# Random-feature attention and a mixture of experts on one core: phases of the feature map computed in bfloat16 parts, with all range reduction on TensorE

## The chip, the cores and the metric

One core of a Trainium2 chip runs the whole program; seven other cores idle. The metric is the device time of one execution in microseconds (us); the lower the better. Before the change the median of six runs is 532.13 us (530.05 to 541.41). A matmul on TensorE (PE) reads its stationary operand by a weight load (PEld) and streams the other; results go to PSUM, which VectorE (DVE) and ScalarE (ACT) empty. GpSimd (POOL) does small work and issues the indirect transfers; SyncE (SP) issues most other transfers.

## The reference

Eight sequences of 512 rows and 128 columns pass attention with 16 heads of 8, a layer norm, a mixture of 8 experts of which each row uses 2, and a second layer norm. All is float32.

```python
def _fourier_kernel(x, proj_mat):
    p = jnp.einsum('blhd,dm->blhm', x, proj_mat) / math.sqrt(D_HEAD)
    return jnp.concatenate([jnp.cos(p), jnp.sin(p)], axis=-1) / math.sqrt(D_KMAP)
q = (x @ Wq.T + bq).reshape(Bv, Lv, N_HEAD, D_HEAD)      # D_HEAD = 8
...
q_prime = _fourier_kernel(q, proj_mat)                    # 128 + 128 features a head
k_prime = _fourier_kernel(k, proj_mat)
kv = jnp.einsum('blhm,blhd->bhmd', k_prime, v)
out = jnp.einsum('blhm,bhmd->blhd', q_prime, kv)
...
x = _layernorm(x + attention(x)); x = _layernorm(x + experts(x))
```

The experts: `relu(x @ W1[e] + b1[e]) @ W2[e] + b2[e]`, weighted by a softmax over the two best of the router's logits.

## The kernel before

**Steps.** The attention of a sequence is cut into 8 steps, 64 in all. Steps 0 to 3 are key steps: each takes 128 rows, and computes the phases p of all 16 heads (128 x 2048 values, in turns: the scale holds a factor 1/(2 pi)), their sines and cosines into a tile `f`, and from them the products with the values (`bank<-f,vm`). After the fourth the sums are transposed into `kv`. Steps 4 to 7 are query steps: each takes 4 heads and all 512 rows, phases again, then `bank<-f,kv`.

**Phases** (`p_phase`, line 546). Keys and queries stand as `kT`, `qT` with (head, dimension) on 128 partitions, in float32. `pbd` holds the projection as a block matrix over 4 heads (32 rows). Four float32 matmuls in four row groups of 32 write four PSUM banks, tiles `p` (two tiles of two banks, line 171). There is one such set: the next step's phases wait until this set is read.

**Range reduction.** A sine needs its argument within half a turn. The constant `TURNED` (line 1476) lists the steps, 0 to 23, in which TensorE does it: after the phases it adds and subtracts a large constant by eight bfloat16 matmuls (`p<-up,once`, `p<-down,once`), so that the bank holds the rounded phase, and subtracts the phases by a second set of float32 matmuls with `npbd`, the negated table. What remains in `p` is minus the fraction. DVE then takes absolute values (`v_abs`, `f<-p` on DVE, two halves) and ACT sines (`v_sin`, `f<-p` on ACT, two halves), and the bank is free. In the other 40 steps ACT rounds (`v_round`, `r<-p,magic`, two halves), DVE subtracts (`v_turn`, `r<-r,p`, two halves), which frees the bank, and from `r` DVE takes absolute values (`f<-r`) and ACT sines (`f<-r`). In both kinds ACT makes the cosines from the absolute values (`f<-f,halfpi`). Two `f` and two `r` tiles exist.

**Experts.** After a sequence's attention its rows are normalized, routed, and scattered by POOL to pages of 128 rows by expert in DRAM (`ys<-y,slot_i`). Pages must first be cleared: SP writes `zero` to them (`ys<-zero`, 19 MB, in the steps 1 to 16). Sequences 0 to 5 form a first group of 55 tiles, 6 and 7 a second of 23. Each tile: SP loads the page (`yg`, 64.5 KB) and the expert's weights (`wst<-wcat`, 322 KB, 6 buffers); TensorE transposes four pages at once (`ident,yg`), does `p_hidden` (`yTg,wst`, four float32 matmuls that the profile counts as eight) and `p_answers` (`w,hT`, likewise); DVE does `hT` and `og` between and after; POOL scatters the answers (`res<-og,yg`). When a group's answers are all there, they are fetched, weighted, normalized and stored.

**The order of the work.** Class `Plan` (line 1342) lays out every task in program order at build time by a list schedule: a task has an engine, an estimated time, predecessors, buffers, and a due time, shifted by kind (`SHIFT`, line 1478). The hardware then runs each engine's instructions strictly in that order (`InOrder`, line 70). All instructions are issued in one helper, so that the profile gives line 78 for nearly all; groups are told apart by the tiles they name. Each class of work uses four PSUM banks (`bank`); after the last step the four phase banks serve too.

Of the kernel before, what the change touches and what calls it, by code (L numbers as in the profile page):

```python
# [18 lines left out]
ROUND = 12582912.0  # L19
# [6 lines left out]
def kernel(  # L26
# [65 lines left out]
    wpool = ctx.enter_context(tc.tile_pool(name="wpool", bufs=6))  # L92
# [24 lines left out]
    first = feat.tile([P, NG * 512], F32, tag="r", name="first")  # L117
    wnat = first[:, 0 : 4 * D].rearrange("p (i d) -> p i d", d=D)
    for i, w in ((1, Wk), (0, Wq), (2, Wv), (3, Wo)):
        nc.scalar.dma_start(out=wnat[:, i, :], in_=w)  # L120
    proj_s = first[0:DH, 4 * D : 4 * D + M]
    sp.dma_start(out=proj_s, in_=proj)
    NB = E * NF
    brow = first[0 : NB + 3, 4 * D + M : 4 * D + M + P]
# [35 lines left out]
    pbd = const.tile([P, NJ * M], F32, name="pbd")  # L160


    npbd = const.tile([P, NJ * M], F32, name="npbd")
# [15 lines left out]
    )  # L179
    mm(P4[3][:, 0:M], heads, proj_s, start=True, stop=True)  # L180
# [11 lines left out]
    bqk = const.tile([P, 2], F32, name="bqk")  # L192


    def p_bcol(bank):
        tr(bank[:, 0 : NB + 3], brow, ident[: NB + 3, : NB + 3])

    def v_bcol(bank):
        dve.tensor_copy(bcol, bank[:, 0 : NB + 3])
        dve.tensor_scalar(bqk, bcol[:, NB : NB + 2], scale, None, ALU.mult)  # L200
# [19 lines left out]

    XW = D + DH
    vm = const.tile([P, NC, NJ * XW], F32, name="vm")
    pool.memset(vm, 0.0)
    kv = const.tile([P, 2, NJ * XW], F32, name="kv")
    pool.memset(kv, 0.0)
# [30 lines left out]
    DY = D + 1  # L258
    zero = const.tile([P, 8, DY], F32, name="zero")
    pool.memset(zero, 0.0)  # L260
    pool.memset(zero[:, :, D:DY].bitcast(I32), 1 << 30)
# [17 lines left out]
    def clear(i, e):  # L279
        n = full[i] if e + 1 < E else NT[i]  # L280
        for t0 in range(0, n, 8):
            k = min(8, n - t0)
            r0 = P * (full[i] * e + t0)
            sp.dma_start(
                out=ys_d[i][r0 : r0 + k * P, :].rearrange("(p k) d -> p k d", k=k),
                in_=zero[:, 0:k, :],
            )
# [56 lines left out]
    class Inverse:  # L344
# [5 lines left out]
        def tile(self, tag):  # L350
            return small.tile([P, NC], F32, tag=tag, name=f"{tag}_{self.name}")
# [8 lines left out]
        def newton(self, eng):  # L360

            rs, ve = self.rs, self.ve
            nw = self.tile("nw")
            eng.tensor_tensor(nw, rs, rs, ALU.mult)
# [61 lines left out]
    def v_rows(bank, r):  # L426
        if r == 0:
            rows8.append(feat.tile([P, NG * 512], F32, tag="r", name="rows8"))
        dve.tensor_copy(rows8[0][:, NG * r * D : NG * (r + 1) * D], bank)
# [7 lines left out]
    def prepare_shift():  # L437
# [10 lines left out]
        for r in range(E // NG):  # L448
# [3 lines left out]
                bank=("rows", r), free=("rows", r), ring=("r", "rows", 2),  # L452
# [3 lines left out]
        plan.give("r", "rows", [t], lag=5)  # L456
        return t

    wr_done, bcol_done = [], []

    def prepare_logits():
        t = plan.add("PE", 0.2, p_bcol, kind="p_bcol", due=-3.5, bank="bcol")
        b = plan.add("DVE", 0.45, v_bcol, kind="v_bcol", due=-3.4, after=[t], bank="bcol", free="bcol")
        bcol_done.append(b)
        t = plan.add("PE", 0.2, p_wo, kind="p_wo", due=-0.5, bank="wo")
# [5 lines left out]
    class Sequence:  # L471
        def __init__(self, b):
# [5 lines left out]
            self.xb = self.z = None  # L478

# [20 lines left out]
        def p_qk(self, i, bank):  # L500
            mm(bank, wT[:, i, 0:D], self.xT, start=True, stop=True)

        def v_qk(self, i, bank, eng):
            t = seq.tile(
                [P, L], F32, tag="qk"[i] + "T", name=f"{'qk'[i]}T_{self.b}", bufs=2 - i
            )
            if eng is dve:
                dve.tensor_scalar(
                    t, bank, bcol[:, NB + i : NB + i + 1], scale, ALU.add, ALU.mult
                )  # L510
            else:
                act.activation(t, bank, AF.Identity, bias=bqk[:, i : i + 1], scale=scale)
            if i:
                self.kT = t
            else:
                self.qT = t
# [29 lines left out]
        def p_phase(self, i, turned):  # L546
            for g in range(NG):
                r0 = 32 * g
                if i < NC:
                    lhs, rhs = self.kT[r0 : r0 + 32, ts(i)], pbd[r0 : r0 + 32, :]  # L550
                else:
                    lhs, rhs = pbd[r0 : r0 + 32, ts(i - NC)], self.qT[r0 : r0 + 32, :]
                mm(P4[g], lhs, rhs, start=True, stop=not turned)
# [13 lines left out]
            for g in range(NG):  # L567
                r0 = 32 * g
                if i < NC:
                    lhs, rhs = self.kT[r0 : r0 + 32, ts(i)], npbd[r0 : r0 + 32, :]  # L570
                else:
                    lhs, rhs = npbd[r0 : r0 + 32, ts(i - NC)], self.qT[r0 : r0 + 32, :]
                mm(P4[g], lhs, rhs, start=False, stop=True)
# [54 lines left out]
        def v_z(self, n, bank):  # L628
            if n == 0:
                self.z = seq.tile([P, NC, D + E], F32, tag="z", name=f"z_{self.b}")  # L630
                self.mv = small.tile([P, NC, 2], F32, tag="mv", name=f"mv_{self.b}")
# [181 lines left out]
        def start_out(self):  # L813
            self.mvo = small.tile([P, NC, 2], F32, tag="mvo", name=f"mvo_{self.b}")
# [5 lines left out]
        def prepare(self):  # L820
# [6 lines left out]
            else:  # L827
# [12 lines left out]
            self.t_k = add("PE", 1.0, lambda bank: self.p_qk(1, bank), kind="p_qk1", due=due + 1, after=[e] + ([before.t_p[NC - 1]] if b else []), bank=("k", b))  # L840
            self.k_done = add(
                "DVE", 0.75, lambda bank: self.v_qk(1, bank, dve), kind="v_qk1", other=("ACT", 0.7, lambda bank: self.v_qk(1, bank, act)), due=due + 1.3,
                after=[self.t_k] + bcol_done, bank=("k", b), free=("k", b),
            )
            self.t_v, self.v_done = [], []
            for n in range(2):
# [9 lines left out]
            self.t_q = add("PE", 1.0, lambda bank: self.p_qk(0, bank), kind="p_qk0", due=due + 4, after=[e] + ([seqs[b - 2].t_p[NS - 1]] if b > 1 else []), bank=("q", b))  # L856
            self.q_done = add(
                "ACT", 0.7, lambda bank: self.v_qk(0, bank, act), kind="v_qk0", other=("DVE", 0.75, lambda bank: self.v_qk(0, bank, dve)), due=due + 4.3,
                after=[self.t_q] + bcol_done,
                bank=("q", b), free=("q", b),  # L860
            )

        def steps(self):
            add = plan.add
            self.t_p, self.t_products = [], []
            for i in range(NS):
                k = NS * self.b + i
                turned = k in TURNED
                s = Step(self, i, turned)
                p = add(  # L870
                    "PE", 2.5 if turned else 1.1, s.p_phase, kind="p_phase", due=k,
                    after=[self.k_done if i < NC else self.q_done], take="p", step=k,
                )
                self.t_p.append(p)
                if turned:
                    a0 = add("DVE", 1.2, lambda s=s: s.v_abs(0), kind="v_abs", due=k + 0.1, after=[p], ring=("f", k, 2))
                    s0 = add("ACT", 1.05, lambda s=s: s.v_sin(1), kind="v_sin", due=k + 0.1, after=[p], ring=("f", k, 2))
                    a1 = add("DVE", 1.2, lambda s=s: s.v_abs(1), kind="v_abs", due=k + 0.1, after=[a0, s0])
                    s1 = add("ACT", 1.05, lambda s=s: s.v_sin(0), kind="v_sin", due=k + 0.1, after=[a0, s0])
# [4 lines left out]
                else:  # L884
                    r0 = add("ACT", 1.1, lambda s=s: s.v_round(0), kind="v_round", due=k + 0.05, after=[p], ring=("r", k, 2))
# [4 lines left out]
                    a = add("DVE", 1.25, lambda s=s: s.v_absolute(), kind="v_absolute", due=k + 1.0, after=[d1], ring=("f", k, 2))  # L890
                    sin = add("ACT", 1.92, lambda s=s: s.v_sine(), kind="v_sine", due=k + 1.2, after=[d1], ring=("f", k, 2))
                    plan.give("r", k, [a, sin])
# [5 lines left out]
                c0 = add("PE", 1.05, lambda bank, s=s: s.p_products(0, bank), kind="p_products", due=k + 2.3, after=sins + need, bank=key)  # L898
                c1 = add("PE", 1.05, lambda bank, s=s: s.p_products(1, bank), kind="p_products", due=k + 2.4, after=[cos, c0], bank=key)
# [5 lines left out]
        def plan_kv(self):  # L905
# [5 lines left out]
                "DVE", 0.6, self.v_kv, kind="v_kv", due=k + 0.5,  # L911
# [618 lines left out]
```

## Time and profile before

| what | us |
|---|---|
| median of six runs | 532.13 |
| the profiled execution | 527.6 |
| its span, first to last instruction | 525.6 |
| first phase matmul | 11.2 |
| steps 0 to 23 (first phase of step 24) | to 146.7 |
| last product of the attention | 397.3 |
| last matmul | 502.8 |
| PE busy | 464.4 |
| DVE busy | 397.2 |
| ACT busy | 358.6 |
| POOL busy | 279.0 |

Busy times are sums over the span; engines work side by side. A row of the profile gives line, engine, operation, the tile written and those read, shapes and count, then busy time and the mean of one. `32*128` behind a matmul is the part of TensorE's array that it uses, rows by columns. PE records are modelled in their ends, so the distance from one start to the next is the better measure of a matmul's cost. Queue names (SPq) stand for the sequencer of an engine, and the granted clock is 1 where TensorE runs at full speed.

### The profile page before, as it was taken

To read this page: it belongs to the slowest core of one execution; us is meant where nothing else is said; L and a number is where in the kernel's file an instruction comes from. 1 tells how busy PE (TensorE), PEld (TensorE's weight loads), DVE (VectorE), ACT (ScalarE), POOL (GpSimd) and SP (SyncE) were. 2 spreads that over 40 slices of the span, in tenths; PEclk is the share of its full clock that TensorE was granted. 3 is DMA by queue.
4 is the path that set the end of the run, shared out by engine and by line. 5 is a ranking of instruction groups with operands and counts; after the bars stand their busy time and mean duration, and the time that the engine had idled before them with its cause. 6 is when DMAs were issued, how large, how long until landed. Compare 5 with 4: busy or idle time off the path is not lost.

```text
span 525.6 us, 13843 instructions
## 1 busy us (share of the span) xinstructions
PE 464.4 (88%) x5107; PEld 306.2 (58%) x5107; DVE 397.2 (76%) x910; ACT 358.6 (68%) x298; POOL 279.0 (53%) x490
## 2 busy tenths in 40 slices
PE   6999999899799999999999999999998659887910
PEld 3654564365247744774676467565757659787910
DVE  3746578479479989998999899999965534298884
ACT  3777887587499999999999999999982100011122
POOL 9300036326316771776377526764773664657685
PEclk9999999999799999999999999999999897989975
DMA  8999857101343117311730263117524545888631
GB/s 205 348 399 351 301 200 286 35 22 53 101 125 94 47 47 194 84 42 54 191 102 31 62 172 101 33 52 206 146 75 132 159 125 164 232 272 261 241 120 61
DMA packets 53110, 77.89 MB, mean 148 GB/s; under 512 B 7896, under 2 KB 31742, under 8 KB 53044
## 3 DMA queue, kind: packets, MB, share of 16 engines
q1 hardware_dynamic: 47604, 68.16, 41.9%
q0 software_dynamic: 4864, 8.60, 5.2%
q8 instruction: 41, 0.67, 0.5%
q10 hardware_dynamic: 576, 0.26, 0.2%
q14 instruction: 25, 0.20, 0.1%
HBM read 41.78 MB, written 34.02 MB: 144 GB/s over the span
## 4 chain that ended last, share of the span: by engine, by line
PE 61%; DVE 14%; issue 6%; ACT 5%; POOL 4%; DMA 4%; another core or an unknown queue 2%; SPq 2%; POOLq 0%; ACTq 0%; DVEq 0%
PE bank L78 40%; PE p L78 22%; ACT f L78 4%; DMA wst<-wcat 3%; DVE r L78 3%; DVE f L78 2%; DVE hT L78 2%; SPq L78 1%; ACT r L78 1%; DVE st L78 1%; POOL rs_o L78 1%; SPq L1174 1%; DVE og L78 1%; POOL res L78 1%
## 5 line engine op out<-in xcount | busy, mean ns | idle before, releaser
L78 ACT ACTIVATE f<-f,halfpi 128x2048 f32<-128x2048 f32 x64 | 128.4, 2006 | 3.7 <-DVE f L78 1.7
L78 POOL DMA_INDIRECT res<-og,yg x78 | 85.8, 1100 | 79.8 <-DVE og L78 55.9
L78 DVE SCALAR_TENSOR_TENSOR r<-r,p 128x1024 f32<-128x1024 f32 x80 | 93.9, 1214 | 6.5 <-ACT r L78 2.5
L78 DVE TENSOR_SCALAR f<-p 128x1024 int32<-128x1024 int32 x48 | 57.2, 1220 | 44.1 <-PE p L78 38.5
L78 ACT ACTIVATE r<-p,magic 128x1024 f32<-128x1024 f32 x80 | 84.6, 1111 | 3.4 <-remote 1.8
L78 POOL DMA_INDIRECT ys<-y,slot_i x64 | 69.4, 1085 | 22.2 <-issue 18.3
L78 ACT ACTIVATE f<-r 128x2048 f32<-128x2048 f32 x40 | 76.5, 1913 | 6.4 <-DVE r L78 4.3
L78 ACT ACTIVATE f<-p 128x1024 f32<-128x1024 f32 x48 | 48.7, 1023 | 29.7 <-PE p L78 17.7
L78 PEld LDWEIGHTS bank<-yTg,wst 128*128 128x128 f32 x464 | 57.3, 198 | 19.3 <-issue 8.3
L78 PEld LDWEIGHTS bank<-f,vm 128*32 128x32 f32 x2048 | 53.5, 110 | 24.6 <-issue 17.1
L78 PE MATMUL bank<-yTg,wst 128*128 128x128 f32 x464 | 63.6, 288 | 4.0 <-DMA wst<-wcat 2.3
L78 PE MATMUL bank<-w,hT 128*128 x464 | 62.6, 281 | 4.9 <-DVE hT L78 3.0
L78 POOL TENSOR_TENSOR xb<-x,bob 128x512 f32<-128x512 f32 x8 | 10.2, 1276 | 106.4 <-DVE z L78 106.4
L78 PE MATMUL bank<-f,vm 128*32 128x128 f32 x2048 | 64.9, 275 | 0.3
L78 PEld LDWEIGHTS bank<-w,hT 128*128 128x128 f32 x464 | 56.6, 193 | 14.2 <-issue 7.1
L78 PE MATMUL bank<-f,kv 128*32 128x512 f32 x512 | 63.0, 602 | 1.8 <-ACT f L78 1.7
L78 PE MATMUL p<-pbd,kT 32*128 32x512 f32 x256 | 46.0, 640 | 4.1 <-DVE r L78 1.9
L78 PE MATMUL p<-qT,pbd 32*128 32x512 f32 x256 | 45.4, 655 | 4.4 <-ACT f L78 4.4
L78 DVE TENSOR_SCALAR f<-r 128x2048 int32<-128x2048 int32 x40 | 48.9, 1222 | 0.4 <-PE bank L78 0.3
L78 DVE TENSOR_TENSOR hT<-bank,wst 128x512 f32<-128x512 f32 x58 | 39.2, 684 | 7.8 <-PE p L78 5.7
L78 PEld LDWEIGHTS bank<-f,kv 128*32 128x32 f32 x512 | 13.2, 109 | 39.3 <-issue 28.0
L78 ACT ACTIVATE yTg<-bank 128x512 f32<-128x512 f32 (+1 forms) x13 | 7.6, 587 | 40.5 <-PE bank L78 33.0
(199 smaller groups left out, 637.1 us busy)
## 6 DMA issues: line engine op xcount, KB each, us to landing
wst<-wcat SPq DMA_DIRECT2D x78, 322.0 KB
ys<-zero SPq DMA_DIRECT2D x36, 516.0 KB
yg<-ys SPq DMA_DIRECT2D x78, 64.5 KB
got<-res SPq DMA_DIRECT2D x6, 512.0 KB
x<-in_L_attn_x_dram SPq DMA_DIRECT2D x8, 256.0 KB
wcat<-in_L_ffn_W_dram SPq DMA_DIRECT2D x8, 256.0 KB
w<-in_L_ffn_W_dram SPq DMA_DIRECT2D x8, 256.0 KB
acc<-y SPq DMA_DIRECT2D x8, 256.0 KB
```

What stands on the lines that cost most here:

```text
L78: ins = getattr(self.engine, op)(*args, **kwargs)
L1174: return nc.values_load(table[0:1, t : t + 1], engines=[engine], min_val=0, max_val=top, skip_runtime_bounds_check_because="a count of pag ...
```

## The change

1. A float32 key, query and projection are each split exactly into three bfloat16 parts (`split`, `split2`: round, subtract, round, subtract), on POOL or DVE, chosen by the planner. Eight of the nine products of parts are kept, each over 8 dimensions: 64 rows a head. The parts of the projection are laid out once on 64 rows, twice over (`sproj`, and `nsproj` negated).
2. The parts of keys and queries must be repeated on those rows: SP stores them to DRAM (`store_parts`, one transfer) and loads them back three, three and two times over (`load_parts`, six transfers, 1 MB), into `ks` and `qs`, one buffer each. The weight's columns are permuted for that (`wP`, `bperm`).
3. `p_phase` works with these: a query step has four bfloat16 matmuls of 64 rows by 512 columns for each table, a key step sixteen of 64 rows by 128 columns, each with weights of its own. Keys of sequence 0 stay as they were (`whole`).
4. `TURNED` is all 64 steps; rounding on ACT and subtracting on DVE fall out.
5. Buffers move: `pbd`, `npbd`, `zero` and the first weights share others' tiles, `wpool` has 7 buffers, memsets of `vm`, `kv` and `zero` go from POOL to DVE, and a page clear is cut into pieces of at most 7 pages (8 before).
6. On DVE the normalization takes 4 instructions for 6; the lists' last step takes 3 for 4.
7. The planner has new estimates, may wait 0.2 us for a task with an earlier due time, and the shifts are others, so the order of nearly everything changes.

```diff
-    wpool = ctx.enter_context(tc.tile_pool(name="wpool", bufs=6))
+    wpool = ctx.enter_context(tc.tile_pool(name="wpool", bufs=7))
...
+    def split(eng, dst, src, left):
+        eng.tensor_copy(dst[:, 0, :], src)
+        eng.tensor_tensor(left, src, dst[:, 0, :], ALU.subtract)
+    def split2(eng, dst, left):
+        eng.tensor_copy(dst[:, 1, :], left)
+        eng.tensor_tensor(dst[:, 2, :], left, dst[:, 1, :], ALU.subtract)
...
+    dve.memset(vm, 0.0)
...
+        def store_parts(self, i):
+            self.parts_d[i] = tc.dram_tile([3, P, L], BF16, name=f"{'qk'[i]}p_d{self.b}")
+            sp.dma_start(out=self.parts_d[i].rearrange("m p n -> p m n"), in_=self.parts[i])
+        def load_parts(self, i):
+            t = seq.tile([P, 2 * NJ, L], BF16, tag="qk"[i] + "s", name=f"{'qk'[i]}s_{self.b}")
+            self.rows_[i] = t
+            src = self.parts_d[i].rearrange("m (s d t) n -> s m d (t n)", s=2, d=DH)
+            for s in range(2):
+                for n in range(3):
+                    k = min(3, NK - 3 * n)
+                    r0 = 64 * s + 24 * n
+                    sp.dma_start(
+                        out=t[r0 : r0 + 8 * k, :, :].rearrange("q t n -> q (t n)"),
+                        in_=src[s, 0:k],
+                    )
...
         def p_phase(self, i, turned):
-            for g in range(NG):
-                r0 = 32 * g
-                if i < NC:
-                    lhs, rhs = self.kT[r0 : r0 + 32, ts(i)], pbd[r0 : r0 + 32, :]
-                else:
-                    lhs, rhs = pbd[r0 : r0 + 32, ts(i - NC)], self.qT[r0 : r0 + 32, :]
-                mm(P4[g], lhs, rhs, start=True, stop=not turned)
+            self.project(i, pbd if self.whole(i) else sproj, True, not turned)
...
+            self.project(i, npbd if self.whole(i) else nsproj, False, True)
+        def whole(self, i):
+            return self.b == 0 and i < NC
+        def project(self, i, table, start, stop):
+            if self.whole(i):
...
+            t = self.rows_[1 if i < NC else 0]
+            for G in range(2):
+                for j in range(NJ) if i < NC else (i - NC,):
+                    for s in range(2):
+                        at, k = slice(64 * s, 64 * s + 64), NJ * G + j
+                        if i < NC:
+                            mm(
+                                P4[2 * G + s][:, ts(j, M)], t[at, k, ts(i)], table[at, :],
+                                start=start and j == 0, stop=stop and j == NJ - 1,
+                            )
+                        else:
+                            mm(P4[2 * G + s], table[at, :], t[at, k, :], start=start, stop=stop)
...
+            last = seqs[b - 1].t_p[NC - 1 if i else NS - 1] if b else None
+            return add("SP", 2.6, lambda: self.load_parts(i), kind="load_parts", due=due, after=[s, last] + sproj_done, land=4)
...
-    HOP = 0.15
+    HOP = 0.07
...
-TURNED = frozenset(range(24))
+TURNED = frozenset(range(64))
```

## Prediction

> **What bounds the kernel now.** I read the page's engine lines first, then busy time by stage, then the instructions in order of time through one step.
>
> ```profile
> PE 464.4 (88%) x5107; PEld 306.2 (58%) x5107; DVE 397.2 (76%) x910; ACT 358.6 (68%) x298; POOL 279.0 (53%) x490
> DMA  8999857101343117311730263117524545888631
> GB/s 205 348 399 351 301 200 286 35 22 53 101 125 94 47 47 194 84 42 54 191 102 31 62 172 101 33 52 206 146 75 132 159 125 164 232 272 261 241 120 61
> ```
>
> PE is busiest, and DMA is full in the first 90 us, where the pages are cleared. By stage (busy us and count of PE, PEld, DVE, ACT, POOL, then granted clock, DMA share, GB/s):
>
> ```profile
> 11.00:147.00 136.00, 128.81 (x1701) 68.03 (x1704) 86.39 (x174) 99.08 (x79) 40.82 (x103) 0.97 0.60 214
> 147.00:272.00 125.00, 120.57 (x1375) 76.43 (x1372) 114.19 (x232) 119.59 (x90) 70.23 (x104) 1.00 0.34 93
> 397.00:432.00 35.00, 25.99 (x205) 24.11 (x199) 17.34 (x61) 3.81 (x8) 19.65 (x32) 0.94 0.50 146
> 432.00:503.00 71.00, 61.10 (x477) 58.56 (x475) 47.54 (x154) 6.76 (x14) 42.77 (x58) 0.91 0.72 221
> 503.00:525.60 22.60, 0.05 (x1) 0.00 (x0) 13.58 (x56) 6.93 (x18) 15.45 (x39) 0.57 0.27 94
> ```
>
> Steps 0 to 23 (turned on TensorE) end at 147. Steps 24 to 63 run to 397 with ACT, PE and DVE all above 90%. From 397 on only experts are left, and ACT rests. A turned step in order of time (start, duration):
>
> ```profile
> 58.46 1.20 PE L78 MATMUL p<-pbd,kT 32*128 32x512 f32 x8
> 59.42 0.45 PE L78 MATMUL p<-up,once 32*128 32x512 bf16 x4
> 59.64 0.45 PE L78 MATMUL p<-down,once 32*128 32x512 bf16 x4
> 59.86 1.09 PE L78 MATMUL p<-npbd,kT 32*128 32x512 f32 x8
> 60.88 1.95 PE L78 MATMUL bank<-f,vm 128*32 128x128 f32 x64
> 61.00 2.35 DVE L78 TENSOR_SCALAR f<-p 128x1024 int32<-128x1024 int32 x2 [1.86 <-PE p L78]
> 62.26 1.02 ACT L78 ACTIVATE f<-p 128x1024 f32<-128x1024 f32 x1 [0.17 <-DVE f L78]
> 63.35 0.75 PE L78 MATMUL p<-pbd,kT 32*128 32x512 f32 x4
> ```
>
> The phases hold PE from 58.46 to 60.88, 2.42 us; DVE and ACT empty them until 63.35, 2.47 us. Only one set of phase banks exists, so a turned step cannot be shorter than 2.42 + 2.47 = 4.89 us; the 24 average (146.7 - 11.2)/24 = 5.65. An unturned step holds PE only 1.07 us but needs two roundings (1.11 each) and a turn (1.21) before its banks come free.
>
> **The change, part by part.** *ACT and DVE in 40 steps.* ACT loses 80 roundings (84.6 us) and 40 long sines (76.5) and gains 80 short sines at 1.023 (82): 79 us less. DVE loses 93.9 + 48.9 and gains 80 absolutes at 1.22 (98): 45 less. Both were above 90% busy in those stages, so PE loses waits there.
>
> *TensorE in 60 steps.* A turned step in 64 rows runs sproj, the eight constant matmuls, nsproj. The row: 512 bf16 columns in four concurrent row groups take 59.64 - 59.42 = 0.22 us. Two halves of 64 rows need two such rounds per table: 0.43. For a query step that is 0.43 + 0.43 + 0.43 = 1.29. To this come switches of the array's tiling. Compare eight fp32 matmuls between others of their own tiling and between other tilings:
>
> ```profile
> 442.65 1.06 PE L78 MATMUL p<-yTg,wst 128*128 128x128 f32 x8
> 443.55 1.06 PE L78 MATMUL bank<-yTg,wst 128*128 128x128 f32 x8
> ...
> 335.06 1.16 PE L78 MATMUL bank<-yTg,wst 128*128 128x128 f32 x8
> 336.15 1.14 PE L78 MATMUL p<-qT,pbd 32*128 32x512 f32 x8
> ```
>
> 0.90 alone, 1.09 among others: 0.2 for a group that stands between two foreign ones. The old step had one such group (2.42 with it); the new one has three, 64 rows, 32 rows, 64 rows. Bounds: 0.2 (inner switches free) to 0.6. I take 0.5, near the row: 1.8 for a query step. The Trainium skill (TensorEngine Tiling (Array Packing), Key Properties) says that changing the tiling mode, not merely the tile, drains TensorE, which speaks against this change and agrees with the 0.2. The page gives no duration; by the row the inner switches make 60 x 0.3 = 18 us of the sum, and they would make none if the rule did not reach half-array tiles.
>
> A key step has 16 matmuls of 128 columns per table, each with weights of its own. Streaming costs 0.22/4 = 0.054 each, so 8 x 0.054 = 0.43 per table if the halves run together, 16 x 0.054 = 0.87 if not. For together speaks that adjacent row groups start 7 ns apart in the trace. That loads cost more is unlikely: the rank matmuls, each with a 128-column bf16 load, start 25 to 38 ns apart. I take 0.55: 0.55 + 0.43 + 0.55 + 0.5 = 2.0 us, bounds 1.5 to 2.8. Another rule of the skill speaks against these steps (TensorE: Matmul & The Clock Gate, The mechanism): a weight load overlaps a running matmul only where the row group differs, and within a half it never differs. Read strictly, with that page's columns/1.2 for a load (107 ns), each matmul of a half would take 0.16, an estimate of 1.3 us per table, 3.5 us per key step and 42 us more than my sum. The rows contradict it: expert matmuls load 128 fp32 columns each in one row group and follow each other at 0.90/8 = 0.11, the streaming time of their two passes.
>
> Phases before: 24 x 2.42 + 40 x 1.07 = 101. After: 4 x 2.42 + 28 x 2.0 + 32 x 1.8 = 123. **TensorE gets 22 us more work**; a gain can only come from idle time: in 4.4 to 503.1 PE was idle 34 us, and at half clock about 7 more were lost (at 430 to 440 the granted clock is 0.55).
>
> *Splits.* 60 instructions on 128x512: 24 stand on DVE (0.68, the hT row: 16 us), 36 on POOL (1.28, the xb row: 46 us). DVE still nets -29; POOL's 53% rises to about 60%. Cover: POOL's idle; if it is gone, page scatters come later by 1.3 each.
>
> *Transfers.* 15 stores (393 KB) and 15 row loads (1.05 MB, six issues each): 21.6 MB more on 77.9, and 105 issues on SP plus 16 smaller clears, at 0.33 each 40 us of SP's time, over some 370 us. A row load waits on SP for the previous sequence's last phase of its kind, and weight and page loads queue behind it; it has four steps (18 us) before it is needed and takes 2.6 us at the 400 GB/s of slice 2. Covered, except at first: up to 90 us some 27 MB move; 5.8 come on top, 83 us at 400 GB/s. I put 2 us on sequence 0's queries, which go through split, store and load while the clears run; bounds 0 to 10.
>
> *Others.* POOL's memsets (4 us) go to DVE's 3.0 us wait at 2.2 to 5.2; bounds 0 to 1. The normalization in four instead of six instructions on DVE and lists of three instead of four instructions save about 1 us at the end. wpool 7: 0 to 2 less.
>
> *The order.* TensorE's program order after: the first expert tile comes in step 27 (24 before), 25.5 tiles lie before the last product (41 before), 52.5 behind (38.5 before). Twenty-nine of these cover the last routing chain (397 to 425), in which PE waited 4.4 and 3.2 us.
>
> **The sum**, on the profiled span of 525.6:
> - Start to first phase: 11.
> - Four old steps at (31.6 - 11.2)/4 = 5.1, plus 2: 23.
> - 23 steps without tiles: floor 1.9 + 2.47 = 4.37. Before, a step was 0.76 above its floor; ACT (4.0 a step) and DVE are then near full, PE less, so 0.65: 23 x 5.0 = 115.
> - 37 steps with 25.5 tiles. PE per step 1.9 + 1.9 products + 0.6 of the sequence's own, per tile 2.1: 163 + 54 = 217. Before: 40 x 3.57 + 41 x 2.1 = 229 in 250, 9% above. With ACT and DVE relieved I take 6%: 230.
> - Tail: 52.5 x 1.92 = 101. Before 74 in 106; without the two long waits and with full clock I take 12 above: 113.
> - End: 22.
>
> 11 + 23 + 115 + 230 + 113 + 22 = 514. The program took 527.6 for the span of 525.6, and the median of the runs is 4.5 above that: 514 + 6.5 = **520 us**, 2% less.
>
> **Rivals** (as medians). *Cheap switches:* inner switches hidden, 1.5 for both kinds of step: 28 x 0.5 + 32 x 0.3 = 24 less, 497. For it: within one tiling fp32 follows bf16 without a gap. Against: the 0.2 row. *Transfers decide:* row loads behind the clears are late by 3 us in three sequences, and the tail, 30.5 MB, gets the 258 GB/s of its 470 to 480 stretch, 118 instead of 113: 520 + 9 + 5 = 534, no change. For it: the DMA line; against: 313 GB/s at 480 to 490. *The halves do not run together (slower):* a key step holds PE 2.8, both in the loop of the banks and in PE's sum: 28 x 0.8 = 22 more, 542. It decides from a key step of 2.0 + 12/28 = 2.43 us. For it: each matmul has its own weights and only 128 columns to hide the load behind; against: the 7 ns. It is also the case in which the packing does not do what it says.
>
> **How the numbers follow.** Forecast 0.50 (its own range 512 to 529), cheap switches 0.12, transfers 0.17, halves in turn 0.21. A measurement tells about 1% from no change, 526.8 to 537.5. Faster: 0.43 of the forecast, 0.12, 0.03: 0.58. Same: 0.07, 0.10, 0.02: 0.19. Slower: 0.23. The range 500 to 541 leaves out about half of each outer case.
>
> **What would show it.** Right: query phases 1.8 and key phases 2.0 from first phase to the next group; steps 5 to 26 about 5.0 apart; last product near 379; last matmul near 492; no ACT rounding. Wrong: key phases above 2.43; phases waiting for the row loads; PE's clock at half in the tail; tiles more than 2.2 apart there.

## The result and the profile after

| | median, us | runs (us) | ratio to before, 95% interval |
|---|---|---|---|
| before | 534.10 | 46 (528.25 to 541.41) | |
| after | 654.11 | 20 (646.94 to 661.63) | 1.226 [1.222, 1.229] |

The change makes the kernel 22.6% slower; the forecast was 520 us, 2% faster. The profiled execution of the changed kernel took 658.2 us, 0.6% above its median; its span is 656.4. First the page: engines, granted clock, DMA.

```profile
PE 493.0 (75%) x5943; PEld 322.3 (49%) x5943; DVE 370.0 (56%) x896; ACT 296.7 (45%) x279; POOL 277.3 (42%) x503
...
PEclk9969687888697799799799898899799799699885
DMA  8756574454236234334136135334236356478822
GB/s 240 263 225 252 229 288 159 135 188 179 69 115 207 80 87 129 123 105 142 67 111 183 52 115 142 109 108 132 78 90 198 102 169 199 114 201 270 254 64 100
```

No engine is near its limit any more: PE falls from 88 to 75% of the span, DVE from 76 to 56, ACT from 68 to 45. And the DMA line has lost its nines: where the clears run, 8, 7, 5, 6 tenths stand instead of 8, 9, 9, 9, and the last packet of a clear ends at 167 us instead of 94. A kernel in which everything has become idler and the time longer is waiting for something with a long latency, not for a resource that is full. By stage (busy us and count of PE, PEld, DVE, ACT, POOL, then granted clock, DMA share, GB/s):

```profile
11.00:147.00 136.00, 92.64 (x1218) 45.87 (x1218) 61.01 (x114) 69.77 (x58) 32.05 (x57) 0.84 0.62 224
147.00:272.00 125.00, 89.09 (x1230) 50.34 (x1229) 68.71 (x157) 69.26 (x59) 47.24 (x76) 0.83 0.39 124
272.00:397.00 125.00, 109.14 (x1640) 64.90 (x1636) 86.27 (x196) 83.40 (x69) 62.23 (x105) 0.95 0.36 113
397.00:485.00 88.00, 79.60 (x940) 47.03 (x936) 54.91 (x118) 50.23 (x41) 36.88 (x56) 0.91 0.37 106
485.00:634.00 149.00, 116.79 (x912) 110.42 (x908) 77.91 (x236) 14.33 (x31) 74.26 (x98) 0.92 0.59 174
634.00:656.40 22.40, 0.48 (x5) 0.29 (x3) 13.44 (x55) 7.09 (x19) 14.83 (x38) 0.53 0.30 106
```

The attention's last product comes at 485 (397 before, 379 forecast), the last matmul at 634 (503; 492). In 11 to 272 PE is busy 182 us of 261, and where it is idle its clock is cut: 0.84 and 0.83 for 0.97 and 1.00. The same 5943 matmuls keep PE busy for 493.0 us here, at a mean clock of 0.877, and for 454.5 us at 0.949 in e11_rows16_told below, which ran on another chip.

The phases themselves are not to blame. A key step in the timeline (start, duration):

```profile
278.74 0.62 PE L78 MATMUL p<-sproj,ks 64*128 64x128 bf16 x16
279.29 0.39 PE L78 MATMUL p<-up,once 32*128 32x512 bf16 x4
279.51 0.38 PE L78 MATMUL p<-down,once 32*128 32x512 bf16 x4
279.83 0.62 PE L78 MATMUL p<-nsproj,ks 64*128 64x128 bf16 x16
280.38 1.95 PE L78 MATMUL bank<-f,vm 128*32 128x128 f32 x64
```

From 278.74 to the next group at 280.38 are 1.64 us, where the forecast had 2.0. What holds the steps up shows in the timeline of the first key step of sequence 1, with SP's six transfers of one row load above it:

```profile
60.23 4.25 SPq L78 DMA_DIRECT2D ks<-kp_d  x6
...
64.52 15.24 SPq L78 DMA_DIRECT2D ys<-zero  x8
...
71.72 0.21 PE L78 MATMUL p<-sproj,ks 64*128 64x128 bf16 x1 [4.06 <-DMA ks<-kp_d]
...
79.52 0.58 PEld L78 LDWEIGHTS <-ks 64*128 64x128 bf16 x12 [7.74 <-issue]
79.55 0.72 PE L78 MATMUL p<-sproj,ks 64*128 64x128 bf16 x10 [7.62 <-DMA ys<-zero]
```

The first matmul waits 4.06 us for one of the six transfers. The next ones wait 7.62 us more; the profile names a clear, but the last packet of the row load, in the DMA records, ends at 79.0, and it is the rows that the matmul reads. From first issue to last packet the 15 row loads take 18.7 to 23.1 us; the ten issued after the last clear still take 19.6 to 22.1. The forecast had 2.6.

### The profile page after: what moved, and what is told of

It is laid out like the page before. It is cut to its first block, busy times and chain, and to the rows that moved or that the text cites. A ratio compares the mean times of both kernels' runs of the same rounds, so it can differ in the third digit from the quotient of the medians.

```text
span 656.4 us, 15660 instructions
## 1 busy us (share of the span) xinstructions
PE 493.0 (75%) x5943; PEld 322.3 (49%) x5943; DVE 370.0 (56%) x896; ACT 296.7 (45%) x279; POOL 277.3 (42%) x503
## 5 line engine op out<-in xcount | busy, mean ns | idle before, releaser
L78 DVE TENSOR_SCALAR f<-p 128x1024 int32<-128x1024 int32 x128 | 153.9, 1220 | 101.4 <-PE p L78 68.4
L78 ACT ACTIVATE f<-p 128x1024 f32<-128x1024 f32 x128 | 129.8, 1023 | 158.9 <-PE p L78 96.9
L78 POOL DMA_INDIRECT res<-og,yg x78 | 77.7, 996 | 119.8 <-DVE og L78 73.0
L78 PE MATMUL bank<-f,vm 128*32 128x128 f32 x2048 | 75.7, 294 | 16.1 <-ACT f L78 11.7
L78 PE MATMUL bank<-f,kv 128*32 128x512 f32 x512 | 70.8, 647 | 2.3 <-DVE kv L78 1.8
L78 PE MATMUL p<-qs,sproj 64*128 64x512 bf16 x128 | 23.0, 410 | 45.0 <-DMA ys<-zero 15.7
L78 PEld LDWEIGHTS <-ks 64*128 64x128 bf16 x896 | 29.0, 101 | 49.0 <-issue 45.4
L78 PE MATMUL p<-sproj,ks 64*128 64x128 bf16 x448 | 20.2, 233 | 26.5 <-DMA ks<-kp_d 10.5
L78 PE MATMUL p<-w,hT 128*128 x192 | 27.8, 294 | 9.2 <-DVE hT L78 7.0
L78 DVE TENSOR_TENSOR og<-bank,wst 128x128 f32<-128x128 f32 x54 | 15.5, 288 | 32.3 <-PE bank L78 16.2
```

Of the source, the lines that this page charges most:

```text
L78: ins = getattr(self.engine, op)(*args, **kwargs)
```

## The experiments

Kernels that share a median of before ran on one chip, beside the kernel before; chips differ, so only ratios are compared across them, and those with care. A ratio without an interval is from one run, or from medians.

| kernel | us | before there | ratio |
|---|---|---|---|
| e1_wide | 621.5 | 543.6 | 1.142 [1.130, 1.155] |
| e2_pieces | 678.8 (one run) | 543.6 | 1.249 |
| e3_once | 598.3 (one run) | 543.6 | 1.101 |
| e4_land19 | 658.0 (one run) | 543.6 | 1.210 |
| e5_rows16 | 609.1 | 541.8 | 1.124 |
| e6_rows16_paced | 582.2 | 541.8 | 1.073 [1.066, 1.080] |
| e7_after_paced | 637.2 (one run) | 541.8 | 1.176 |
| e8_fp32_turned | 613.8 (one run) | 541.8 | 1.133 |
| e9_before_paced | 513.7 | 506.7 | 1.015 [1.013, 1.017] |
| e10_rows16_early | 546.2 | 506.7 | 1.077 [1.071, 1.083] |
| e11_rows16_told | 533.6 | 506.7 | 1.056 [1.052, 1.060] |
| e12_fp32_paced | 547.4 (one run) | 506.7 | 1.080 |
| e13_one_pause | 578.7 | 533.5 | 1.081 [1.074, 1.088] |
| e14_whole1 | 574.4 | 533.5 | 1.076 [1.069, 1.083] |
| e15_whole2 | 566.3 | 533.5 | 1.061 [1.054, 1.068] |
| e16_whole1_nopause | 581.1 | 533.5 | 1.080 [1.070, 1.090] |
| e17_whole2_paced | 518.3 | 508.0 | 1.012 [1.006, 1.018] |
| e18_whole2_early | 532.6 | 508.0 | 1.048 [1.043, 1.053] |

### Why a row load takes 20 us

In the trace a row load is 128 packets of 8 KB, each 0.31 us at the median, and at most five overlap although six transfers are under way. The Trainium skill (DMA: Bandwidth & Descriptors, Why a DMA increments its semaphore by 16 and not by 1) says that a transfer runs on k of the 16 engines, the largest k up to 16 that divides the slowest dimension of both its access patterns, and on the lowest-numbered ones. The six transfers have outermost dimensions of 3 and 2: by that rule all of them share engines 0 to 2, and the busiest moves 6 x 8 packets, an estimate of 48 x 0.31 = 15 us plus the issues. That is near the 18.7 to 23.1 measured, and it can be tested (the records don't say which engine carried a packet). Theory A: the outermost dimension decides. A2: the size of the pieces does. B: the loads wait in the queues behind clears and expert weights. C: the order itself or the splits cost the time, and the loads only end last.

*e1_wide* stores eight copies, and loads each half of 64 rows with 8 outermost:

```diff
-            self.parts_d[i] = tc.dram_tile([3, P, L], BF16, name=f"{'qk'[i]}p_d{self.b}")
-            sp.dma_start(out=self.parts_d[i].rearrange("m p n -> p m n"), in_=self.parts[i])
+            self.parts_d[i] = tc.dram_tile([NK, P, L], BF16, name=f"{'qk'[i]}p_d{self.b}")
+            for r in range(NK):
+                sp.dma_start(out=self.parts_d[i][r], in_=self.parts[i][:, r % 3, :])
...
+                sp.dma_start(
+                    out=t[64 * s : 64 * s + 64, :, :].rearrange("q t n -> q (t n)"), in_=src[s]
+                )
```

> Edit: the eight copies of the parts are written to DRAM one below the other (8 stores of 128 rows by 1 KB for 1 of 384 rows), and loaded back by two transfers of 64 rows, whose outermost dimension is 8, for six of 24 or 16 rows, whose outermost dimension is 3 or 2. Tasks, estimates and order as in the changed kernel. Theory A (the row loads are slow because a transfer runs on as many DMA engines as its outermost dimension allows, 3 and 2 here, always the same ones): packets of 8 KB then run on 8 engines, a load takes some 5 to 7 us instead of 17 to 20, the waits of the phases for their rows shrink to a few us in sum, and the time falls from 654 to about 540 (the 92 us of the attention come back, the 45 us behind it only in part). Theory B (the loads wait behind page clears and expert weights in the queues): the bytes are more (stores 1.05 MB for 0.39), a load stays at 15 us or more, and the time stays above 630.

A load lands after 10.7 to 13.1 us and the kernel gains 8 points of 23. The direction is A's; landing and time miss what A had put on them.

*e2_pieces* pads the row tile by 8 columns, so that each transfer falls into pieces of 1 KB with the outermost 3 and 2 kept.

> Edit: the row tile gets 8 spare columns, so that a load cannot be written as whole 8 KB rows and goes in pieces of 1 KB; the six transfers, their bytes and their outermost dimensions of 3 and 2 stay. Theory A (engines by the outermost dimension): still three engines, 1024 pieces of 0.046 us with 384 on the busiest engine, 17 to 20 us a load, time 640 to 665. Theory A2 (engines by the number or size of pieces): 192 pieces a transfer spread over 16 engines, 4 to 6 us a load, time about 540.

Still 20 to 24 us in most loads, and 678.8 us, in its one run even above the 640 to 665 of A: A2 falls.

*e5_rows16* puts (head half, dimension) outermost in DRAM, so that one transfer of 128 rows does it:

```diff
+            self.parts_d[i] = tc.dram_tile([16, NK, NJ * 2, L], BF16, name=f"{'qk'[i]}p_d{self.b}")
+            for n in range(3):
+                k = min(3, NK - 3 * n)
+                for m in range(k):
+                    sp.dma_start(out=self.parts_d[i][:, 3 * n + m], in_=self.parts[i][:, m, :])
...
+            sp.dma_start(
+                out=t.rearrange("q t n -> q (t n)"),
+                in_=self.parts_d[i].rearrange("g r t n -> (g r) (t n)"),
+            )
```

> The rows are stored as [16, 8, 8, 512] in DRAM, with (head pair group, dimension) outermost, by eight stores of 128 KB, and loaded by one transfer of 128 rows of 8 KB; the program order of the engines stays that of the changed kernel. Theory (a row load uses as many DMA engines as its outermost dimension allows): 8 packets of 0.31 us on each of 16 engines, so a load lands 4 to 6 us after its issue, the waits for rows (2_5, 3_1, 4_1, 5_1) fall away, and the time is that of the kernel that loads the rows only once, 590 to 610 us. Rival (the rows are late for another reason, such as the store before them or the queue): loads still above 9 us and the time above 615.

B falls with the loads after the clears, which are no faster in the changed kernel (19.6 to 22.1 us). Here loads land after 7.0 to 9.6 us beside the clears and 4.4 to 8.3 after them (4.4 to 4.7 in the last five). With 3 or 2, 8 and 16 outermost the same 1 MB takes some 20, 12 and 4.5 us, and at most 5, 11 and 19 packets overlap. The number of transfers falls too, from six to two to one, but six that ran each on its own share of the engines would show more than five packets at once: A is shown. The time, 609, is at the upper end of what was expected.

*e3_once* loads rows only once, queries of sequence 0 and keys of sequence 1; every later phase uses these, splits and stores stay:

```diff
+            if i in first_rows:
+                self.rows_[i] = first_rows[i]
+                return
```

> Left out: the rows are loaded only once, queries for sequence 0 and keys for sequence 1; all later sequences take their phases from these rows. The splits and stores stay. Theory A and theory B: without the later loads the phases never wait for rows but twice at the start; the attention ends near 385 instead of 485, time 535 to 555. Theory C (the loss is in the searched order itself or in the splits on POOL and DVE, and the loads only end last): the time stays above 600.

598.3, in one run: without any later row load 10 points of the 22.6 are still there. That is far above the 535 to 555 of A and B, and just below the 600 of C; there was a second cause. *e4_land19* tells the planner 4.2 us of issue and 19 of landing:

> Edit: only the planner's estimates of the row load: it lands after 19 us (4 before) and holds SP for 4.2 (2.6 before), as measured; the transfers are those of the changed kernel and the order is laid out anew with the same shifts. Theory A with one row tile for each kind: the load still takes 18 us and must fit into the four steps of the other kind, so the planner can only put expert tiles into the waits: 600 to 640. Rival: the misjudged landing is all there is, the order heals it: below 560.

658 us, in one run, above both expectations (1.210 of before, against 1.226): the order that the planner makes from the true landing does not hide the 20 us. That no order could, with one row buffer for each kind, is not shown.

### A run of page scatters stops the other engines

With the loads out of the way, a handful of steps of 10 to 17 us stood in both e3_once and e5_rows16, at the same places of the program (2_1, 3_7, 5_7, 7_5), and each beside a run of POOL's page scatters. A step is named by sequence and number, and its time here and below is the distance from the first phase matmul of the step before it to its own. Here e5_rows16 between the phases of 3_6 and those of 3_7:

```profile
212.52 0.96 POOL L78 DMA_INDIRECT ys<-y,slot_i  x1 [0.31 <-issue]
...
212.70 0.60 PE L78 MATMUL p<-qs,nsproj 64*128 64x512 bf16 x4
...
213.24 3.34 PE L78 MATMUL bank<-f,kv 128*32 128x512 f32 x21
...
217.37 1.05 PE L78 MATMUL bank<-f,kv 128*32 128x512 f32 x3 [0.79 <-issue]
...
219.51 0.38 PE L78 MATMUL bank<-ident,x 128*128 128x128 f32 x2 [0.44 <-issue]
...
220.13 0.98 POOL L78 DMA_INDIRECT res<-og,yg  x1 [0.30 <-issue]
220.92 0.27 PE L78 MATMUL bank<-yTg,wst 128*128 128x128 f32 x1 [1.03 <-issue]
...
223.23 1.02 ACT L78 ACTIVATE f<-p 128x1024 f32<-128x1024 f32 x1 [10.18 <-remote]
223.24 2.35 DVE L78 TENSOR_SCALAR f<-p 128x1024 int32<-128x1024 int32 x2 [9.17 <-remote]
```

The phases end at 213.3. DVE and ACT have nothing else to do and start on them at 223.2. In between POOL sends scatters every 1.27 us, up to 221.1, and from 216 on PE, which waits for nothing that the profile names, starts a matmul or a few every 0.7 us ("issue"). The DMA engines are not full meanwhile: their share is 0.16 in 211 to 216 us and 0.13 in 216 to 224. A "remote" or "issue" wait of 10 us on three engines at once is the line to look for. *e6_rows16_paced* breaks these runs by a small power on POOL (1.04 us on 128x4), with the program order unchanged:

```diff
         def scatter(self, k, c):
+            if c % 2 == 0:
+                pool.tensor_tensor(gap_, small_wide(one), small_wide(mhalf), ALU.pow)
             pool.indirect_dma_start(
```

> As the kernel with rows on 16 engines, and POOL computes a small power (1.04 us on 128x4) ahead of every second page scatter, so that no more than two scatters follow each other at 1.27 us. Program order unchanged, POOL 33 us busier. Theory (a run of eight scatters at 1.27 us holds up TensorE and what its completions release, from the fifth on): the steps 2_1, 3_7, 5_7, 7_5 and the wait after the attention's last scatters shrink from 10 to 16 us to 5 to 7, VectorE and ScalarE start on the phases within 1 us of their end as in the kernel before, and the time is 30 to 55 us below the unpaced one: 545 to 575. Rival (the scatters follow each other because the others wait, not the other way round): the long steps stay, and the time is within 1% of the unpaced one or above.

(The loop runs over c outside and k inside, so the pauses came to stand ahead of the 1st, 2nd, 5th and 6th scatter; up to three follow each other.) The same place in its timeline:

```profile
211.16 0.61 PE L78 MATMUL p<-qs,nsproj 64*128 64x512 bf16 x4
...
211.70 2.78 PE L78 MATMUL bank<-f,kv 128*32 128x512 f32 x24
...
212.56 0.96 POOL L78 DMA_INDIRECT ys<-y,slot_i  x1 [0.30 <-issue]
...
213.54 1.05 POOL L78 TENSOR_TENSOR gap<-one,mhalf 128x4 f32<-128x4 f32 x1
214.34 1.02 ACT L78 ACTIVATE f<-p 128x1024 f32<-128x1024 f32 x1 [2.84 <-PE bank L78]
214.35 2.36 DVE L78 TENSOR_SCALAR f<-p 128x1024 int32<-128x1024 int32 x2 [1.59 <-PE bank L78]
```

DVE and ACT start 0.8 us after POOL's pause begins, and PE goes on at its pace. The four long steps (us, from start to start):

| step | e5_rows16 | e6_rows16_paced |
|---|---|---|
| 2_1 | 11.6 | 6.1 |
| 3_7 | 14.0 | 6.6 |
| 5_7 | 12.4 | 5.6 |
| 7_5 | 16.7 | 5.7 |

The kernel gains 27 us of 609, with 33 us more work on POOL and both on one chip; that is a little less than the 30 to 55 expected. That the runs hold up the core, and not the other way round, is shown; through what in the chip they do it is not. Pauses alone in the changed kernel:

> The changed kernel with nothing but the small power ahead of every second page scatter. Theory of the scatters: 30 to 55 us less than the changed kernel, 600 to 625; rival: 645 or more.

637 in one run against the 645 or more of the rival, but less than expected: 17 us below the changed kernel's median elsewhere (5 points in ratio). Many of its runs fall into the waits for rows, which may be why; that is not shown.

Why did the kernel before suffer less? Its timeline has, within one run of scatters:

```profile
231.80 1.73 POOL L78 DMA_INDIRECT ys<-y,slot_i  x1 [0.30 <-issue]
...
232.20 1.22 DVE L78 TENSOR_SCALAR f<-r 128x2048 int32<-128x2048 int32 x1
...
237.62 1.54 POOL L78 DMA_INDIRECT ys<-y,slot_i  x1 [0.30 <-issue]
237.82 1.22 DVE L78 TENSOR_SCALAR f<-r 128x2048 int32<-128x2048 int32 x1
```

A scatter that meets DVE's absolute values from `r` takes 1.5 to 2.0 us instead of 0.96: these instructions pause POOL for free, in five of its eight runs. The Trainium skill (SBUF — State Buffer, Who interferes with whom) has a reason for the pause: some DVE instructions between SBUF operands lock GpSimd out of a shared port, so it can't write descriptors. The trace agrees: 10 of 64 page scatters take above 1.3 us before, all ten beside an `f<-r`, which only one of the 54 others meets; after, where all absolutes read PSUM, 2 of 64 do. Two of the three runs that stay whole in the kernel before, at 88 and 128 us, lie among its turned steps, and long steps stand there too: 2_1, 2_7 and 3_0 take 7.6, 8.2 and 8.2 us, all others up to 3_0 4.8 to 6.4. *e8_fp32_turned* makes all steps such steps, without any bf16 part: the kernel before with one line changed, `TURNED = frozenset(range(64))`.

> The kernel before with one edit: all 64 steps are turned on TensorE, in float32 (no parts, no rows, no new transfers, its own shifts). TensorE gets 40 x (2.42 - 1.07) = 54 us more phases; ACT and DVE are relieved as in the changed kernel. By TensorE's sum alone 575 to 590. With the theory of the scatters the absolutes now all read PSUM, nothing paces the scatters any more, six more runs of scatters go unbroken, and 20 to 40 us come on top: 600 to 625. Rival (relief of ACT and DVE pays, TensorE had slack): 545 to 560.

613.8, in one run, and none of its page scatters takes over 1.2 us: nothing breaks the runs. With the pauses (*e12_fp32_paced*, on another chip):

> The kernel before with all steps turned on TensorE in float32, and the small power ahead of every second page scatter. Theory of the scatters: 30 to 45 us less than without the pauses, 570 to 585, which is TensorE's sum alone. Rival: 605 or more.

The ratio falls from 1.133 to 1.080, the size expected (the absolute number is of a faster chip, and each is one run). Steps 4_1, 5_1, 5_7, 6_5 and 7_7 take 11 to 17 us without the pauses and 6 to 8 with them; 5_3, 6_3 and 6_7 are long in both, for another reason. So moving the range reduction alone, with no bf16 part, brings long steps of the same kind. How much of this gain is due to the pauses is less sure than in e6: no kernel without them was profiled on e12's chip. The kernel before with pauses, *e9_before_paced*:

> The kernel before with nothing but the small power (1.04 us on POOL) ahead of every second page scatter, program order unchanged. Before has three runs of eight scatters without a pause (at 88, 128 and 420 us of its profile), of which the later two hold TensorE below 3 matmuls a microsecond for some 5 us; the other runs are paused by POOL's own longer scatters (1.7 us). Theory of the scatters: 2 to 10 us less than before, with up to 4 us lost at 397 to 425 where the last sequence's pages wait for their scatters. Rival (the runs cost before nothing): the same or 1 to 5 us more.

A miss: 1.5% slower. Steps 2_1, 2_7 and 3_0 now take 5.3, 5.6 and 5.3 us, as the theory has it (on another chip), but the whole is longer. Where it loses the time is open. The pauses may push the answers' scatters back where DVE already breaks the runs; that is not shown.

### What is left

*e10_rows16_early* sets the shift of page loads to -1.95 as before (34 tiles before the last product instead of 25); *e11_rows16_told* also tells the planner 5.3 us for the stores, 0.7 + 7 for the load and 2.35 for a scatter with its pause.

> As the paced kernel with rows on 16 engines, and the shift of page loads is -1.95 as in the kernel before instead of 13.4, so that 34 tiles instead of 25 stand before the last product. If the order is what still costs (a tile in the tail 2.75 us, in the attention hidden): 15 to 25 us less, 557 to 567. If a tile costs TensorE 2.1 to 2.3 us in the attention too: within 1% of 582, less by 5 at most.

> As the paced kernel with rows on 16 engines, and the planner is told what the trace shows: 5.3 us of SP for the eight stores, 0.7 for the load, 7 us from issue to landing, 2.35 us of POOL for every second page scatter; page loads shifted by 5 so that 32 tiles stand before the last product. If what remains over the kernel before is work laid out by wrong durations (waits for rows of 7 us, steps of 9 to 11): 550 to 570. Rival (a busy TensorE sets it): 575 to 590.

Earlier tiles alone give nothing: 1.077 and 1.073, on two chips. True durations, with 32 tiles ahead, give 2 points on the same chip as e10, a ratio between the two expectations. In e11's trace steps 0_4, 1_1, 1_4 and 1_5 still take 8 to 14 us: the rows for 0_4 and 1_4 land 1.6 and 0.5 us before their phases, and ahead of 1_1 and 1_5 DVE stands still for 8.0 and 8.1 us until a store of parts, among the clears in SP's queue, is out. So sequence 0, and then 0 and 1, were given back to float32 phases (`whole` returns `self.b < WHOLE`, 1 and 2), with one pause of the four kept:

> As the kernel whose planner was told the durations, with one power of 1.04 us per sequence, between the fourth and the fifth page scatter, instead of four (these stood ahead of the 1st, 2nd, 5th and 6th). If only a run of more than four holds TensorE up: 1.045 to 1.06 of before, as POOL has 25 us less to do and answers go out sooner. Rival (runs of four and the answers' scatters behind them hold it up as well): 1.07 or more.

> As the kernel with one pause; sequence 0 computes its queries' phases in float32 too, as its keys, so that no rows are needed before step 8 and one store and load less cross the clears; stores and loads are due 6 and 4.6 steps earlier. If rows behind the clears are what is left: steps 0_4 to 1_1 at 5 us instead of 8 to 14, some 20 us less, 1.00 to 1.025 of before. Rival (TensorE's work sets the end): 1.04 or more.

> As the one above with sequences 0 and 1 in float32 (TensorE 8 x 0.8 = 6 us more), first row load at some 90 us, when most clears are out. If rows of sequence 1 still wait behind clears in the kernel above: 1 to 2% below it. If they don't: 1% above it.

> As the kernel with sequence 0 in float32, its one pause left out, same program order. Theory of the scatters: runs of eight at 1.27 us return and hold TensorE up, 3 to 6% over the kernel with the pause. Rival (the order has changed so much that the runs cost nothing): within 1%.

Four kernels on one chip: 1.081, 1.076, 1.061, 1.080. The waits for rows are gone in e15 but for one of 4.0 us (steps 1_4 and 1_5 take 5.3 and 5.7), worth 2 points together, less than half of what was expected. One pause in the middle is nearly worth nothing (1.076 against 1.080, intervals overlap): in e13 and e14 runs of four, with answers' scatters behind them, still give steps of 12 to 19 us. My "only more than four" is wrong. So the last pair has a pause ahead of the 1st, 3rd, 5th and 7th scatter (`if k == 0`), two in a row at most:

> As the kernel with sequences 0 and 1 in float32, with a power of 1.04 us ahead of the 1st, 3rd, 5th and 7th page scatter instead of the 5th alone, told to the planner. Theory of the scatters: the gain of four pauses over one, 2.5 points, comes back: 1.03 to 1.045 of before, steps 3_7, 4_0, 6_6 and 6_7 below 8 us. Rival (runs of three or four cost nothing, the gap between those kernels was the chip): 1.055 or more.

> As the one above with page loads and first expert products due earlier (shifts -6), so that 39 of 78 tiles stand before the last product, as in the kernel before (40). If the tiles moved behind the attention are what remains: 1.00 to 1.02. If a tile costs TensorE its 2 us wherever it stands: within 1% of the one above.

```profile
PE 456.0 (89%) x5943; PEld 308.5 (60%) x5943; DVE 365.1 (71%) x889; ACT 296.4 (58%) x278; POOL 304.9 (59%) x531
...
PEclk9999999999998999999999999999999999979965
DMA  7999936987594772566674653575456696868341
```

That is the page of e17_whole2_paced: PE at 89%, clock at nine tenths nearly throughout, the nines back in the DMA line. It is 1.2% [0.6, 1.8] slower than before, better than the 1.03 to 1.045 expected: with rows on 16 engines, true durations, two float32 sequences and pauses, nearly all of the 22.6% is gone. That its chip is another one than e15's leaves the share of the pauses in these last 5 points uncertain. e18, with 39 tiles before the last product, is 3.6 points slower: both expectations missed, and moving tiles ahead of the last product in this way does not recover what remained. Its steps 3_7, 6_0 and 7_3 take 14 to 19 us; ahead of 3_7 six tiles' products stand in one row (11 us) between a step's phases and its own products. No kernel here beats the one before.

## Why the prediction was wrong

**The phases (right in kind, too dear).** Forecast 2.0 and 1.8 us a step; measured 1.65 and 1.62 (1.73 at most in 46 of the 60; the others hold waits). The two halves run together, and the inner switches of tiling are nearly hidden: two rounds of 0.22 per table and the constants give 1.3, so 0.3 is left for all switches, where I took 0.5. TensorE's phases cost 4 x 2.4 + 28 x 1.65 + 32 x 1.62 = 108 us, not 123. The rival of the halves in turn decides from 2.43 and is out. The rival of cheap switches had the price nearly right and forecast 497.

**The row loads (the step that failed first).** That one "takes 2.6 us at the 400 GB/s of slice 2" priced six transfers by the bytes of sixteen engines. The diff showed the shapes, `src[s, 0:k]` with k of 3 and 2. The term measured 18.7 to 23.1 us, beyond the "four steps (18 us)" that should cover it; steps 1_5, 2_5, 4_1 and 5_1 take 12 to 18 us after, and 4.6 to 4.9 in e3_once. The attention ends at 485.4 with the loads and at 430.7 without (e3_once, on another chip): 55 us. The rival in which transfers decide named the right wait, with 3 us in three sequences; its price was as wrong as mine. The sign that the prediction itself gave for being wrong, phases waiting for the row loads, came true.

**POOL ("Cover: POOL's idle").** POOL's own time did not grow (277.3 us busy, 279.0 before), so its idle was not gone. I asked what POOL's work costs POOL, and never what DVE's removed work did for others. Taking the roundings and turns from ACT and DVE was costed as pure relief; the `f<-r` instructions that went with them had been breaking the runs of scatters. In e6 against e5 the attention ends at 415.6 instead of 436.7: 21 us of the term "37 steps with 25.5 tiles".

**The tail (mis-sized).** 52.5 tiles at 1.92 plus 12 make 113; it took 149, 2.81 a tile. Before it took 2.76 (104.9 us for 38 tiles), so a tile had become hardly slower: I had priced a tile by PE's busy time and taken the waits out by argument. The row of before to use was the tail's own length over its tiles: 52.5 x 2.76 = 145.

**The end** was 22 us, as forecast. The sum misses by 106 us in the attention and 36 in the tail. Of the 106, 55 and 21 are named above, from different kernels, so they need not add; for the rest e11 and e15 point at rows and stores behind the clears and an order laid out with wrong durations, and the stage table at PE's granted clock of 0.84 and 0.83; how much belongs to each is not separated.

## What to carry to other kernels

Price a transfer by its shape before its bytes: look at the outermost dimension of both sides, and at how many packets overlap in a trace. When work is taken off an engine, ask what that work was slowing down, and whether something depends on it. Price a stage by its own length per unit in the trace, waits included, unless a measurement shows that a wait goes.

## What the runs showed of the hardware

- Runs of indirect scatters at 1.27 us hold back TensorE (a few matmuls every 0.7 us) and the start of DVE and ACT on its results, by up to 10 us; both resume 0.8 to 2.1 us after POOL stops. In e6 pauses of 1 us took four long steps from 12 to 17 us to 5.6 to 6.6; one pause in the middle of a run gained nothing clear of noise (e14, e16). Answers' scatters at 1.28 us in the tail, seventeen in a row in e17, did not do it: PE stays busy 25.5 of 28 us there.
- The same 1 MB from DRAM to 128 partitions takes some 20, 12 or 4.5 us with 3 or 2, 8 or 16 and more outermost; 1 KB instead of 8 KB pieces, with 3 or 2 outermost, made it no faster.
- TensorE steps between 64-row, 32-row and 64-row tilings cost 0.3 us in 1.6 at most, and sixteen matmuls of 128 columns with weights of their own cost no more than four of 512: 0.55 to the next group for either.
- Chips differ: the kernel before has medians of 507 to 544 us on the five that it ran on beside the experiments, so that ratios from different chips carry some points of doubt.
